# Fourier attention with routed experts: turning the phases of every step on TensorE from bfloat16 parts

## The chip, the cores and the metric

One NeuronCore of a Trainium2 chip runs the kernel. The metric is device time in microseconds (us), the median of 15 executions: 506.96 us before the change (504.1 to 509.99).

## The reference, cut to what matters

```python
# x: (8, 512, 128); 16 heads of 8; proj: (8, 128)
q = (x @ Wq.T + bq); k = (x @ Wk.T + bk); v = (x @ Wv.T + bv)
p = einsum('blhd,dm->blhm', q or k, proj) / sqrt(8)       # the phases
q_, k_ = concat([cos(p), sin(p)], -1) / sqrt(128)         # 256 features a head
kv = einsum('blhm,blhd->bhmd', k_, v); a = einsum('blhm,bhmd->blhd', q_, kv)
x = layernorm(x + a @ Wo.T + bo)
# 8 experts 128 -> 512 -> 128 with relu; each row goes to its best 2 of 8 by a softmax router
x = layernorm(x + sum_e routed[e] * (relu(x @ W1[e] + b1[e]) @ W2[e] + b2[e]))
```

## The kernel before, in words

**Attention.** A sequence (512 rows) is done in 8 steps: four make k features (one per chunk of 128 rows, all heads), four make q features (one per j of the four heads of each group of 32 channels, all rows). A step has 128 x 2048 phases in four banks of PSUM (`P4`, two halves `PH`), held by one step at a time. `p_phase` (line 546) multiplies a float32 block of 32 channels by the block-diagonal projection `pbd`, one matmul a bank, the four on four groups of 32 rows of the array. Phases are counted in turns, and must be brought to half a turn around zero before the sine. In a *turned* step (the first 24 of 64, `TURNED`, line 1476) TensorE does that: two bfloat16 matmuls a bank, `up` and `down`, add and take away a large constant (what is left is the phase rounded to whole turns), and the same float32 product with `npbd`, the negative projection, is added. `v_abs` on VectorE and `v_sin` on ScalarE then read PSUM, a half at a time. In the other 40 steps `p_phase` makes the product only; ScalarE adds the rounding constant (`v_round`, into the tile `r`), VectorE subtracts (`v_turn`), and absolute value (`v_absolute`) and sine (`v_sine`) are taken from `r` in SBUF, the whole step at once. In both, `v_cos` takes the cosine from the absolute value, in place. `products` (line 575) multiplies the features by v or by the summed kv.

**Experts.** After a sequence's attention come `v_aT`, `p_z`, `stats`, `Inverse` (power, then `newton`), the router (`v_route0` to `v_rank`), and GpSimd's indirect scatters of each row and its slot number into pages of 128 rows in DRAM (`ys`). Sequences 0 to 5 form group 0 (55 page loads), 6 and 7 group 1 (23). A page is loaded (`load`), its expert's W1, biases and shift row are loaded into one of six buffers of `wpool` (`weights`), and `p_hidden`, `v_max`, `p_answers`, `v_answers` and a scatter to `res` follow. When a group is done, `fetch`, `combine` (or `weigh` and `total`), a second layer norm and the store follow. Before rows are scattered, the pages are cleared from the tile `zero` (`clear`, line 279): 38 transfers of SP's queue, eight pages or fewer each.

**What sets the order.** Each engine works through its instructions in the order in which they are issued. `Plan.make` (line 1378) works that order out beforehand: a task has an engine, a cost in us, tasks that it waits for, buffers that it takes from rings, and a due time, shifted by the table `SHIFT`. Some tasks can go to either of two engines. The costs are numbers written in the code; nothing on the chip follows them except the order. SP's queue is also such an order: weights, pages, clears and stores wait behind one another.

Of the kernel before, what the change touches and what calls it, by code (L numbers as in the profile page):

```python
# [25 lines left out]
def kernel(  # L26
# [32 lines left out]
    P = 128  # L59
# [32 lines left out]
    wpool = ctx.enter_context(tc.tile_pool(name="wpool", bufs=6))  # L92
# [24 lines left out]
    first = feat.tile([P, NG * 512], F32, tag="r", name="first")  # L117
    wnat = first[:, 0 : 4 * D].rearrange("p (i d) -> p i d", d=D)
    for i, w in ((1, Wk), (0, Wq), (2, Wv), (3, Wo)):
        nc.scalar.dma_start(out=wnat[:, i, :], in_=w)  # L120
    proj_s = first[0:DH, 4 * D : 4 * D + M]
    sp.dma_start(out=proj_s, in_=proj)
    NB = E * NF
    brow = first[0 : NB + 3, 4 * D + M : 4 * D + M + P]
# [35 lines left out]
    pbd = const.tile([P, NJ * M], F32, name="pbd")  # L160


    npbd = const.tile([P, NJ * M], F32, name="npbd")
# [15 lines left out]
    )  # L179
    mm(P4[3][:, 0:M], heads, proj_s, start=True, stop=True)  # L180
# [11 lines left out]
    bqk = const.tile([P, 2], F32, name="bqk")  # L192


    def p_bcol(bank):
        tr(bank[:, 0 : NB + 3], brow, ident[: NB + 3, : NB + 3])

    def v_bcol(bank):
        dve.tensor_copy(bcol, bank[:, 0 : NB + 3])
        dve.tensor_scalar(bqk, bcol[:, NB : NB + 2], scale, None, ALU.mult)  # L200
# [19 lines left out]

    XW = D + DH
    vm = const.tile([P, NC, NJ * XW], F32, name="vm")
    pool.memset(vm, 0.0)
    kv = const.tile([P, 2, NJ * XW], F32, name="kv")
    pool.memset(kv, 0.0)
# [30 lines left out]
    DY = D + 1  # L258
    zero = const.tile([P, 8, DY], F32, name="zero")
    pool.memset(zero, 0.0)  # L260
    pool.memset(zero[:, :, D:DY].bitcast(I32), 1 << 30)
# [17 lines left out]
    def clear(i, e):  # L279
        n = full[i] if e + 1 < E else NT[i]  # L280
        for t0 in range(0, n, 8):
            k = min(8, n - t0)
            r0 = P * (full[i] * e + t0)
            sp.dma_start(
                out=ys_d[i][r0 : r0 + k * P, :].rearrange("(p k) d -> p k d", k=k),
                in_=zero[:, 0:k, :],
            )
# [56 lines left out]
    class Inverse:  # L344
# [5 lines left out]
        def tile(self, tag):  # L350
            return small.tile([P, NC], F32, tag=tag, name=f"{tag}_{self.name}")
# [8 lines left out]
        def newton(self, eng):  # L360

            rs, ve = self.rs, self.ve
            nw = self.tile("nw")
            eng.tensor_tensor(nw, rs, rs, ALU.mult)
# [61 lines left out]
    def v_rows(bank, r):  # L426
        if r == 0:
            rows8.append(feat.tile([P, NG * 512], F32, tag="r", name="rows8"))
        dve.tensor_copy(rows8[0][:, NG * r * D : NG * (r + 1) * D], bank)
# [7 lines left out]
    def prepare_shift():  # L437
# [10 lines left out]
        for r in range(E // NG):  # L448
# [3 lines left out]
                bank=("rows", r), free=("rows", r), ring=("r", "rows", 2),  # L452
# [3 lines left out]
        plan.give("r", "rows", [t], lag=5)  # L456
        return t

    wr_done, bcol_done = [], []

    def prepare_logits():
        t = plan.add("PE", 0.2, p_bcol, kind="p_bcol", due=-3.5, bank="bcol")
        b = plan.add("DVE", 0.45, v_bcol, kind="v_bcol", due=-3.4, after=[t], bank="bcol", free="bcol")
        bcol_done.append(b)
        t = plan.add("PE", 0.2, p_wo, kind="p_wo", due=-0.5, bank="wo")
# [5 lines left out]
    class Sequence:  # L471
        def __init__(self, b):
            self.b = b
            self.g = group_of(b)
            self.m = b - gstart[self.g.i]

            self.hurry = b >= B - 2
            self.xb = self.z = None

# [20 lines left out]
        def p_qk(self, i, bank):  # L500
            mm(bank, wT[:, i, 0:D], self.xT, start=True, stop=True)

        def v_qk(self, i, bank, eng):
            t = seq.tile(
                [P, L], F32, tag="qk"[i] + "T", name=f"{'qk'[i]}T_{self.b}", bufs=2 - i
            )
            if eng is dve:
                dve.tensor_scalar(
                    t, bank, bcol[:, NB + i : NB + i + 1], scale, ALU.add, ALU.mult
                )  # L510
            else:
                act.activation(t, bank, AF.Identity, bias=bqk[:, i : i + 1], scale=scale)
            if i:
                self.kT = t
            else:
                self.qT = t
# [29 lines left out]
        def p_phase(self, i, turned):  # L546
            for g in range(NG):
                r0 = 32 * g
                if i < NC:
                    lhs, rhs = self.kT[r0 : r0 + 32, ts(i)], pbd[r0 : r0 + 32, :]  # L550
                else:
                    lhs, rhs = pbd[r0 : r0 + 32, ts(i - NC)], self.qT[r0 : r0 + 32, :]
                mm(P4[g], lhs, rhs, start=True, stop=not turned)
# [13 lines left out]
            for g in range(NG):  # L567
                r0 = 32 * g
                if i < NC:
                    lhs, rhs = self.kT[r0 : r0 + 32, ts(i)], npbd[r0 : r0 + 32, :]  # L570
                else:
                    lhs, rhs = npbd[r0 : r0 + 32, ts(i - NC)], self.qT[r0 : r0 + 32, :]
                mm(P4[g], lhs, rhs, start=False, stop=True)
# [54 lines left out]
        def v_z(self, n, bank):  # L628
            if n == 0:
                self.z = seq.tile([P, NC, D + E], F32, tag="z", name=f"z_{self.b}")  # L630
                self.mv = small.tile([P, NC, 2], F32, tag="mv", name=f"mv_{self.b}")
# [181 lines left out]
        def start_out(self):  # L813
            self.mvo = small.tile([P, NC, 2], F32, tag="mvo", name=f"mvo_{self.b}")
# [5 lines left out]
        def prepare(self):  # L820
# [19 lines left out]
            self.t_k = add("PE", 1.0, lambda bank: self.p_qk(1, bank), kind="p_qk1", due=due + 1, after=[e] + ([before.t_p[NC - 1]] if b else []), bank=("k", b))  # L840
            self.k_done = add(
# [688 lines left out]
```

## Time and profile before

| what | us |
|---|---|
| median of 15 runs | 506.96 |
| the profiled execution, its own time | 507.4 |
| its span, first to last instruction | 505.3 |
| TensorE busy | 451.5 (89%) |
| VectorE busy | 397.9 (79%) |
| ScalarE busy | 358.1 (71%) |
| GpSimd busy | 278.7 (55%) |
| moved by DMA | 77.89 MB, mean 154 GB/s |

The views used here: the busy time of each engine in chosen stretches (columns: stretch, its length, then for each engine busy us and number of instructions, the granted TensorE clock, DMA share, GB/s); groups of instructions by form (count, then union of busy us, mean ns of one, and idle before); the timeline (start, length, engine, instruction, count of instructions merged in the line). PE is TensorE, PEld its weight loads, DVE VectorE, ACT ScalarE, POOL GpSimd, SP the engine that issues most DMAs. Ends of matmuls are modelled, so the cost of a piece of PE work is read from its start to the next piece's start. A float32 matmul shows as two matmul instructions, a bfloat16 one as one.

### The profile page before, as it was taken

How to read it: one execution, taken by the hardware profiler on the slowest of the kernel's cores; microseconds unless marked ns; L12 is line 12 of the kernel's file. 1: busy time of each engine (PE TensorE's matmuls, PEld its weight loads, DVE VectorE, ACT ScalarE, POOL GpSimd, SP SyncE). 2: the span in 40 equal slices, each digit the busy share in tenths (PEclk: the TensorE clock that was granted, in tenths of full speed). 3: DMA queues.
4: the chain of work that ended last, by engine and by line, in shares of the span. 5: the costliest groups of instructions: out<-in, count | busy, mean ns of one | idle time of the engine just before them, and what ended most of it. 6: DMA issues, size and time to landing. Idle time of an engine off the chain costs nothing.

```text
span 505.3 us, 13843 instructions
## 1 busy us (share of the span) xinstructions
PE 451.5 (89%) x5107; PEld 300.5 (59%) x5107; DVE 397.9 (79%) x910; ACT 358.1 (71%) x298; POOL 278.7 (55%) x490
## 2 busy tenths in 40 slices
PE   6999999999999999999999999999999697687910
PEld 3664564365267545764765567566657687687910
DVE  3845669579698999999999999999984564478884
ACT  3876887877899999999999999999992100011122
POOL 9300026526426862675577537764784577357685
PEclk9999999999999999999999999998999899899975
DMA  7999757301433035312531343027434576877631
GB/s 199 343 399 398 282 201 277 111 23 55 145 107 113 27 91 153 106 34 83 160 106 38 110 130 105 31 59 215 130 96 142 161 224 177 285 242 228 197 117 64
DMA packets 53110, 77.89 MB, mean 154 GB/s; under 512 B 7896, under 2 KB 31742, under 8 KB 53044
## 3 DMA queue, kind: packets, MB, share of 16 engines
q1 hardware_dynamic: 47604, 68.16, 42.8%
q0 software_dynamic: 4864, 8.60, 5.3%
q8 instruction: 41, 0.67, 0.6%
q10 hardware_dynamic: 576, 0.26, 0.2%
q14 instruction: 25, 0.20, 0.1%
HBM read 41.78 MB, written 34.02 MB: 150 GB/s over the span
## 4 chain that ended last, share of the span: by engine, by line
PE 57%; DVE 16%; ACT 8%; DMA 7%; issue 6%; POOL 4%; SPq 1%; POOLq 0%; ACTq 0%; DVEq 0%
PE bank L78 36%; PE p L78 21%; ACT f L78 4%; DVE r L78 4%; ACT r L78 3%; DMA wst<-wcat 3%; DVE f L78 2%; DVE hT L78 2%; DMA ys<-y,slot_i 1%; DMA got<-res 1%; DMA res<-og,yg 1%; DVE acc L78 1%; DVE st L78 1%; POOL rs_o L78 1%; DVE og L78 1%
## 5 line engine op out<-in xcount | busy, mean ns | idle before, releaser
L78 ACT ACTIVATE f<-f,halfpi 128x2048 f32<-128x2048 f32 x64 | 128.7, 2011 | 3.2 <-DVE f L78 1.2
L78 POOL DMA_INDIRECT res<-og,yg x78 | 86.5, 1108 | 70.6 <-DVE og L78 43.5
L78 DVE SCALAR_TENSOR_TENSOR r<-r,p 128x1024 f32<-128x1024 f32 x80 | 93.8, 1213 | 4.9 <-ACT r L78 4.8
L78 ACT ACTIVATE r<-p,magic 128x1024 f32<-128x1024 f32 x80 | 84.8, 1117 | 0.0
L78 DVE TENSOR_SCALAR f<-p 128x1024 int32<-128x1024 int32 x48 | 56.8, 1219 | 33.1 <-PE p L78 30.5
L78 POOL DMA_INDIRECT ys<-y,slot_i x64 | 69.5, 1085 | 22.3 <-issue 17.2
L78 ACT ACTIVATE f<-r 128x2048 f32<-128x2048 f32 x40 | 76.8, 1919 | 4.5 <-DVE r L78 3.5
L78 PEld LDWEIGHTS bank<-yTg,wst 128*128 128x128 f32 x464 | 57.4, 200 | 18.6 <-issue 6.8
L78 PEld LDWEIGHTS bank<-f,vm 128*32 128x32 f32 x2048 | 53.3, 110 | 24.0 <-issue 19.5
L78 PE MATMUL bank<-yTg,wst 128*128 128x128 f32 x464 | 63.5, 289 | 3.1 <-ACT yTg L78 1.6
L78 ACT ACTIVATE f<-p 128x1024 f32<-128x1024 f32 x48 | 49.1, 1024 | 23.9 <-PE p L78 17.0
L78 PE MATMUL bank<-f,vm 128*32 128x128 f32 x2048 | 64.2, 275 | 0.1
L78 POOL TENSOR_TENSOR xb<-x,bob 128x512 f32<-128x512 f32 x8 | 10.2, 1277 | 96.3 <-DVE z L78 96.3
L78 PE MATMUL bank<-w,hT 128*128 x464 | 60.8, 279 | 2.0 <-DVE hT L78 2.0
L78 PE MATMUL bank<-f,kv 128*32 128x512 f32 x512 | 61.9, 599 | 0.4 <-ACT f L78 0.4
L78 PEld LDWEIGHTS bank<-w,hT 128*128 128x128 f32 x464 | 55.6, 192 | 11.0 <-issue 4.1
L78 DVE TENSOR_SCALAR f<-r 128x2048 int32<-128x2048 int32 x40 | 49.0, 1225 | 0.1
L78 PE MATMUL p<-pbd,kT 32*128 32x512 f32 x256 | 44.2, 643 | 2.3 <-DVE r L78 1.0
L78 PE MATMUL p<-qT,pbd 32*128 32x512 f32 x256 | 43.4, 640 | 1.7 <-ACT f L78 1.7
L78 DVE TENSOR_TENSOR hT<-bank,wst 128x512 f32<-128x512 f32 x58 | 39.2, 683 | 3.0 <-PE p L78 1.2
L78 ACT ACTIVATE yTg<-bank 128x512 f32<-128x512 f32 (+1 forms) x13 | 7.6, 587 | 40.7 <-PE bank L78 40.7
L78 PEld LDWEIGHTS bank<-f,kv 128*32 128x32 f32 x512 | 13.3, 109 | 36.1 <-issue 25.4
(199 smaller groups left out, 625.9 us busy)
## 6 DMA issues: line engine op xcount, KB each, us to landing
wst<-wcat SPq DMA_DIRECT2D x78, 322.0 KB
ys<-zero SPq DMA_DIRECT2D x36, 516.0 KB
yg<-ys SPq DMA_DIRECT2D x78, 64.5 KB
got<-res SPq DMA_DIRECT2D x6, 512.0 KB
x<-in_L_attn_x_dram SPq DMA_DIRECT2D x8, 256.0 KB
wcat<-in_L_ffn_W_dram SPq DMA_DIRECT2D x8, 256.0 KB
w<-in_L_ffn_W_dram SPq DMA_DIRECT2D x8, 256.0 KB
acc<-y SPq DMA_DIRECT2D x8, 256.0 KB
```

What stands on the lines that cost most here:

```text
L78: ins = getattr(self.engine, op)(*args, **kwargs)
```

## The change

All 64 steps are turned. Except for the k steps of sequence 0 (`whole`), the projection is made from bfloat16 parts. `v_split` and `v_split2` write q or k as three bfloat16 parts that sum to it; the projection's parts are laid out once as `sproj` and `nsproj` in 64 rows: 8 products of parts by 8 channels of a head. For that the parts must stand in other rows: `store_parts` writes them to DRAM (two transfers), `load_parts` reads them back in runs of 24, 24 and 16 rows for each half of 64 (six transfers) as `rows_`. `project` then multiplies 64-row blocks, two halves of the array: four matmuls of 512 columns for a q step, sixteen of 128 columns for a k step, once with `sproj` and once with `nsproj`. Weight columns and biases of q and k are permuted to match (`wP`, `bperm`).

The tile `r` goes; `zero`, `first`, `rows8` and `pbd` move into the rings of other tiles, `wpool` has seven buffers. Clears go to GpSimd's queue, seven pages or fewer each (54 of them), planned four at a time by a ring of the plan. VectorE, not GpSimd, clears `vm`, `kv` and `zero` at the start. `newton` on VectorE takes four instructions and not six. The planner's costs, its rules for choosing among ready tasks and `SHIFT` are changed.

```diff
-    wpool = ctx.enter_context(tc.tile_pool(name="wpool", bufs=6))
+    wpool = ctx.enter_context(tc.tile_pool(name="wpool", bufs=7))
...
+    def split(eng, dst, src, left):
+        eng.tensor_copy(dst[:, 0, :], src)
+        eng.tensor_tensor(left, src, dst[:, 0, :], ALU.subtract)
+    def split2(eng, dst, left):
+        eng.tensor_copy(dst[:, 1, :], left)
+        eng.tensor_tensor(dst[:, 2, :], left, dst[:, 1, :], ALU.subtract)
...
+    vm = const.tile([P, NC, NJ * XW], F32, name="vm")
+    dve.memset(vm, 0.0)
+    kv = const.tile([P, 2, NJ * XW], F32, name="kv")
+    dve.memset(kv, 0.0)
+    zero = keep.tile([P, 7, DY], F32, tag="got", name="zero", bufs=3)
+    dve.memset(zero, 0.0)
...
-            sp.dma_start(
-                out=ys_d[i][r0 : r0 + k * P, :].rearrange("(p k) d -> p k d", k=k),
+    def clear(i, r0, k):
+        pool.dma_start(
+            out=ys_d[i][r0 : r0 + k * P, :].rearrange("(p k) d -> p k d", k=k),
+            in_=zero[:, 0:k, :],
+        )
...
+            if eng is dve:
+                self.nb = self.tile("nb")
+                dve.tensor_tensor(nw, rs, rs, ALU.mult)
+                dve.scalar_tensor_tensor(nw, nw, -0.5, ve, ALU.mult, ALU.mult)
+                dve.scalar_tensor_tensor(rs, nw, 1.5, rs, ALU.add, ALU.mult)
+                dve.scalar_tensor_tensor(self.nb, self.mv[:, :, 0], -1.0, rs, ALU.mult, ALU.mult)
+                return
...
+        def v_split(self, i, eng):
+            self.parts[i] = seq.tile(
+                [P, 3, L], BF16, tag="parts", name=f"{'qk'[i]}p_{self.b}", bufs=1
+            )
+            split(eng, self.parts[i], self.qk[i], self.qk[i])
+        def v_split2(self, i, eng):
+            split2(eng, self.parts[i], self.qk[i])
+        def store_parts(self, i):
+            self.parts_d[i] = tc.dram_tile([2, 3, P // 2, L], BF16, name=f"{'qk'[i]}p_d{self.b}")
+            for s in range(2):
+                sp.dma_start(
+                    out=self.parts_d[i][s].rearrange("m r n -> r m n"),
+                    in_=self.parts[i][64 * s : 64 * s + 64, :, :],
+                )
+        def load_parts(self, i):
+            t = seq.tile([P, 2 * NJ, L], BF16, tag="qk"[i] + "s", name=f"{'qk'[i]}s_{self.b}")
+            self.rows_[i] = t
+            src = self.parts_d[i].rearrange("s m (d t) n -> s (m d) (t n)", d=DH)
+            for s in range(2):
+                for n in range(3):
+                    k = min(3, NK - 3 * n)
+                    r0 = 64 * s + 24 * n
+                    sp.dma_start(
+                        out=t[r0 : r0 + 8 * k, :, :].rearrange("q t n -> q (t n)"),
+                        in_=src[s, 0 : 8 * k],
+                    )
...
+            self.project(i, pbd if self.whole(i) else sproj, True, not turned)
...
+            self.project(i, npbd if self.whole(i) else nsproj, False, True)
+        def whole(self, i):
+            return self.b == 0 and i < NC
+        def project(self, i, table, start, stop):
...
+            t = self.rows_[1 if i < NC else 0]
+            for G in range(2):
+                for j in range(NJ) if i < NC else (i - NC,):
+                    for s in range(2):
+                        at, k = slice(64 * s, 64 * s + 64), NJ * G + j
+                        if i < NC:
+                            mm(
+                                P4[2 * G + s][:, ts(j, M)], t[at, k, ts(i)], table[at, :],
+                                start=start and j == 0, stop=stop and j == NJ - 1,
+                            )
+                        else:
+                            mm(P4[2 * G + s], table[at, :], t[at, k, :], start=start, stop=stop)
...
+        def split(self, i, t, due):
+            t = add(
+                "POOL", 2.3, lambda: self.v_split(i, pool), kind="v_split", due=due, after=[t], ring=("parts", (b, i), 1),
+                other=("DVE", 1.1, lambda: self.v_split(i, dve)),
+            )
+            t = add(
+                "POOL", 2.3, lambda: self.v_split2(i, pool), kind="v_split2", due=due, after=[t],
+                other=("DVE", 1.1, lambda: self.v_split2(i, dve)),
+            )
+            s = add("SP", 0.8, lambda: self.store_parts(i), kind="store_parts", due=due, after=[t], land=2.6)
+            last = seqs[b - 1].t_p[NC - 1 if i else NS - 1] if b else None
+            return add("SP", 4.0, lambda: self.load_parts(i), kind="load_parts", due=due, after=[s, last] + sproj_done, land=4.5)
...
+                one_ = 1.14 if self.whole(i) else 0.65
                 p = add(
-                    "PE", 2.5 if turned else 1.1, s.p_phase, kind="p_phase", due=k,
+                    "PE", 2 * one_ + 0.2 if turned else one_, s.p_phase, kind="p_phase", due=k,
...
+                "POOL", 0.6, lambda i=i, r0=r0, k=k: clear(i, r0, k), kind=f"clear{i}",
+                due=0.3 * n + 8 * i, land=6, ring=("clear", n, 4),
...
-    HOP = 0.15
+    HOP = 0.07
-    SETUP = {"PE": 6.4, "ACT": 6.9, "DVE": 7.0, "POOL": 14.0, "SP": 17.0}
+    SETUP = {"PE": 5.75, "ACT": 6.8, "DVE": 6.7, "POOL": 11.6, "SP": 16.2}
+    WAIT = 0.2
+    EARLY = {"PE": 0.14, "ACT": 0.1, "DVE": 0.09, "POOL": 0.0, "SP": 0.0}
...
-TURNED = frozenset(range(24))
+TURNED = frozenset(range(64))
```

## The prediction

> **What bounds the kernel now.** I read the busy time by stretches first, since no mean over the span says what a change of one stage is worth. I cut the span where the turned steps end (136 us), where attention ends (379), and where the last matmul ends (482.6).
>
> ```profile
> 0.00:30.00 30.00, 24.86 (x324) 15.28 (x325) 17.08 (x29) 17.98 (x17) 16.35 (x83) 1.00 0.96 291
> 30.00:136.00 106.00, 104.35 (x1388) 53.61 (x1386) 74.18 (x155) 83.84 (x68) 34.64 (x68) 1.00 0.54 199
> 136.00:160.00 24.00, 22.75 (x287) 15.04 (x286) 20.48 (x37) 22.24 (x17) 9.75 (x18) 1.00 0.41 130
> 160.00:379.00 219.00, 215.44 (x2429) 137.10 (x2425) 207.17 (x421) 215.21 (x159) 138.23 (x192) 0.99 0.35 99
> 379.00:482.60 103.60, 84.10 (x693) 79.48 (x685) 65.51 (x216) 12.01 (x23) 64.14 (x92) 0.97 0.67 204
> 482.60:505.30 22.70, 0.00 (x0) 0.00 (x0) 13.47 (x56) 6.83 (x18) 15.64 (x38) 0.59 0.27 93
> ```
>
> The columns are PE, PEld, DVE, ACT, POOL, clock, DMA share, GB/s. Stage A (to 136, 24 turned steps) is PE's: 104.35 of 106.00 us, ACT at 79%. Stage B (136 to 379, 40 unturned steps) has PE at 98%, ACT at 98%, DVE at 94%. Stage C is the experts' tail: PE at 81%, DMA share 0.67. Stage D is the last layer norm and store.
>
> PE and ACT both look full in B; the groups by form tell which one leads.
>
> ```profile
> L78 ACT ACTIVATE f<-f,halfpi 128x2048 f32<-128x2048 f32 x64 | 128.7, 2011 | 3.2 <-DVE f L78 1.2
> L78 DVE SCALAR_TENSOR_TENSOR r<-r,p 128x1024 f32<-128x1024 f32 x80 | 93.8, 1213 | 4.9 <-ACT r L78 4.8
> ...
> L78 ACT ACTIVATE r<-p,magic 128x1024 f32<-128x1024 f32 x80 | 84.8, 1117 | 0.0
> L78 ACT ACTIVATE f<-r 128x2048 f32<-128x2048 f32 x40 | 76.8, 1919 | 4.5 <-DVE r L78 3.5 <-PE bank L78 0.8
> ...
> L78 DVE TENSOR_SCALAR f<-p 128x1024 int32<-128x1024 int32 x48 | 56.8, 1219 | 33.1 <-PE p L78 30.5 <-ACT f L78 2.5
> ```
>
> An unturned step costs ACT 2 x 1.117 + 1.919 + 2.011 = 6.16 us; 40 of them are 246 us, and B lasts 243 (neighbours overlap a little). ACT sets B. The PE timeline shows the price of both kinds of step, read from start to next start.
>
> ```profile
> 62.38 1.19 PE L78 MATMUL p<-pbd,kT 32*128 32x512 f32 x8
> 63.34 0.44 PE L78 MATMUL p<-up,once 32*128 32x512 bf16 x4
> 63.55 0.44 PE L78 MATMUL p<-down,once 32*128 32x512 bf16 x4
> 63.77 1.08 PE L78 MATMUL p<-npbd,kT 32*128 32x512 f32 x8
> 64.78 1.95 PE L78 MATMUL bank<-f,vm 128*32 128x128 f32 x64
> 66.67 0.73 PE L78 MATMUL bank<-wT,aT 128*128 128x136 f32 x4
> 67.33 1.14 PE L78 MATMUL p<-pbd,kT 32*128 32x512 f32 x8
> ```
>
> One float32 projection is 0.96 to 1.01 us; up and down together 0.43; a turned step's phases 62.38 to 64.78 = 2.40; its products 1.89; the period 4.95. In B the same form lasts longer, because it is held up between banks that ACT and DVE have not left:
>
> ```profile
> 255.81 2.15 PE L78 MATMUL p<-qT,pbd 32*128 32x512 f32 x8
> 257.89 2.05 PE L78 MATMUL bank<-yTg,wst 128*128 128x128 f32 x16
> ```
>
> The phases take 59.3 busy us in B (29.13 on qT, 30.18 on kT, the stretches of those tiles), against 40 x 1.14 = 45.6 when they run freely. So 13.7 us of PE's 238.2 in B are waits, and its work there is 224.5.
>
> **The change, part by part.** *New projections.* The trace has no matmul on 64 rows. For a q step, four matmuls of 512 columns run two at a time. The nearest row is up/down: four of 512 columns on four row groups in 0.215 us. Two pairs are then 0.43 (0.86 if the halves do not run together), and a q step is 0.43 + 0.43 + 0.43 = 1.29. For a k step, sixteen matmuls stream the same columns, 0.43, but each loads 128 columns of weights. Below: the products pay 1.89 / 64 = 29.5 ns for a matmul with its own load of 32 columns, 0.47 for sixteen. Above: the experts' float32 matmuls, full array, 128 columns loaded each, go eight in 0.89 us, 111 ns each, 1.78 for sixteen. I take 0.55, near the lower row, since loads into one half of the array can lie beside a matmul in the other, as up/down's four groups do: a k step is 2 x 0.55 + 0.43 = 1.53.
>
> The Trainium skill speaks against this ("TensorE: Matmul & The Clock Gate", "LDWEIGHTS (loading the stationary operand)"): a load costs its columns / 1.2 ns, however few its rows, 107 ns here. This trace's bfloat16 loads of 128 columns (`once`) average 93 ns, of the same size. By the page, with two halves loading side by side, sixteen would be an estimated 0.85 us, and the sum below some 17 us higher.
>
> *Stage A.* Four k steps of sequence 0 stay at 2.40. Of the other 20, eight are k steps (2.40 - 1.53 = 0.87 each) and twelve q steps (1.11 each): 7.0 + 13.3 = 20.3 us, all of it where PE is the limit. What is late next: ACT's 2 x 1.024 + 2.011 = 4.06 a step and the loop phases, two `v_abs` (2 x 1.219), phases, some 4.0. A's steps last (136 - 10)/24 = 5.25 us with their fillers, 4.40 afterwards, so both stay below. **-20.3.**
>
> *Stage B.* ACT loses 40 x (6.16 - 4.06) = 84 us and stops being the bound. DVE loses 40 x (2 x 1.213 + 1.225 - 2 x 1.219) = 48.5 of its 227.7 and gains the splits of ten tiles. A split is four passes of 128x512. The rows bound a pass between 0.31 (a quarter of the 1.225 us pass over 2048 elements in SBUF) and 0.68 (`hT`, 512 from PSUM); I take the code's 2.2 a tile, 22 us; DVE falls to 201. On GpSimd a pass is 1.28 (`xb`, 128x512); it is busy 148 of 243 in B and has room. PE becomes the bound: 20 k steps x (1.53 - 0.97) + 20 q steps x (1.29 - 0.97) = +17.6; 224.5 + 17.6 = 242.1. At the packing of A (104.35/106, 98.4%) that takes 246 us against 243. **+3.** So the 84 us of ACT buy almost nothing here: the bound moves over to PE, which was nearly full.
>
> *Start.* q of sequence 0 is needed at step 4, 30.6 us. Its parts go behind the loads on SP's queue (last issued at about 18 us) while DMA runs at a share of 0.96. Store and load are 0.39 + 1.05 MB; nearby landings are 3.1 us (`res`) and 5.7 (the chain's longest `got`). 18 + 3.1 + 5.7 = 27 at best; doubled under load, 36. A stall of 0 to 5; I take **+2**. VectorE's memsets cost GpSimd 1.97 + 1.06 + 1.02 before; DVE waits for the projection until 4.8 us anyway, so they are hidden there; without that cover, up to 2.
>
> *Later returns.* 15 tiles x 1.44 MB = 21.6 MB on 77.9; DMA share is 0.54 in the rest of A, 0.35 in B. A tile may load as soon as its predecessor's four steps are over, and has the other kind's four steps, 16 us, to land. SP gets 120 issues of 0.4 to 0.7 us (48 to 84) and loses 38 clears of 1.2 us (46). Nothing, as long as SP's order holds; behind a waiting `load_parts` stand the weights of the next pages, whose seven buffers cover some 15 us.
>
> A second rule speaks against it ("DMA: Bandwidth & Descriptors", "Why a DMA increments its semaphore by 16 and not by 1"): a transfer uses the largest number of engines up to 16 that divides its rows, so 12 for 24 rows. No run here shows it yet. By it four of the six transfers would last a third longer, an estimated 2 us on a 5.7 us landing, inside the 16 us of cover.
>
> *Clears.* 54 on GpSimd at 0.6 (its plain transfers: 522 to 614 ns) are 32 us, most between 20 and 60 us, where GpSimd is busy 0.00 and 0.00. Nothing; in another place they would hold scatters.
>
> *Tail.* Two waits on the weights in the chain of C are 5.9 and 5.0 us; a seventh buffer lets a load start one page sooner (103.6/38 = 2.7 us): 0 to -5.4, I take -3. The shorter `newton`, once on the last chain, -0.4. **-3.4.**
>
> Sum: 507.4 - 20.3 + 3 + 2 - 3.4 = 488.7 on the profiled execution's own time, which stands 0.1% above the median of 506.96. **Forecast 489.**
>
> **Rivals.** (1) *The loads of the k steps' weights are the bound.* 28 k steps x 2 projections. From 57 ns a matmul (0.91 a projection) the gain is gone: 28 x 2 x 0.36 = 20. Halfway between both rows, 72 ns, 1.16 a projection: 28 x 1.22 = +34, **523**, slower than before. For it: 111 ns is the only row with loads of 128 columns for each matmul. Against: those are float32 and hold the whole array. (2) *The parts come back late.* SP's fixed order meets landings longer than planned, 1 us more for each of 14 returns and 5, not 2, at the start: 488.7 + 14 + 3 = **506**, no change to measure. For it: DMA at 0.96 at the start, chain waits of 5 to 6 us on weights. Against: 16 us of cover. (3) *Splits hold PSUM.* 30 half splits of 1.1 us stand in DVE's order before a `v_abs`, which alone frees PSUM for the next phases; if a quarter shows on PE, +8: **497**. For it: DVE at 94% in B. Against: GpSimd has room, and DVE falls to 201. (4) *PE's slack in C closes too.* Held-back pages fill the 19.5 us that PE idles there, and ACT's freedom lets B run at 100%: 489 - 4 - 10 = **475**.
>
> **How the numbers follow.** Forecast 0.50 (480 to 499), (1) 0.14, (2) 0.10, (3) 0.10, (4) 0.16. About 0.3% is what a measurement can tell from no change. Faster: 0.50 + 0.16 + 0.10 and a little of (2), 0.78; same 0.04, slower 0.18 from (1) and the rest of (2). The range reaches to (4) and past (2), with all low ends (0.43 a projection -6.7, start -2, tail -2.4, and part of (4)) giving 470, and the break-even of (1) plus half its price 514.
>
> **What would show it.** Mean steps of 4.4 us in A instead of 5.25; phases of a q step at 1.3 and of a k step at 1.5 from start to start (above 2.2: rival 1); ACT below 75% and PE above 97% in B; attention ending near 360; no PE idle that a `qs` or `ks` load ends (else 2); no PE wait on a split (else 3). Wrong altogether if PE's work grows by more than 20 us or SP's queue holds the weights.

## The result, and the profile after

The changed kernel takes **537.9 us** (median of 9 runs, 534.6 to 539.9) against 506.4 (46 runs): a ratio of **1.062** (95% interval 1.060 to 1.064). The forecast was 489 with a range to 514: the change was to make the kernel faster, and made it slower. The profiled span is 535.3 us, 30.0 more than before. Some runs of a kernel are slower than others without a reason that a trace gives; ratios, and the differences worked out from them, leave out runs over 1.5% above the fastest of their kernel, medians do not.

The page of the kernel after, first its busy times and then the rows of TensorE's busy share and of DMA (40 slices, tenths):

```profile
PE 454.6 (85%) x5943; PEld 306.4 (57%) x5943; DVE 375.0 (70%) x912; ACT 293.4 (55%) x275; POOL 298.5 (56%) x539
...
PE   5985998959974999999998999999989999789700
...
DMA  7998799595489945674556467423787776859131
```

ScalarE lost 65 us and VectorE 23, as the change promises; TensorE is as busy as before (451.5) and idles 27 us more. The stretches, cut where attention (366 us) and the last matmul (509.1) end now; columns as in the prediction (PE, PEld, DVE, ACT, POOL, clock, DMA share, GB/s):

```profile
0.00:30.00 30.00, 22.57 (x175) 12.86 (x175) 18.28 (x44) 10.69 (x10) 20.75 (x99) 1.00 0.94 301
30.00:136.00 106.00, 88.31 (x1478) 48.21 (x1472) 71.58 (x141) 78.11 (x66) 53.56 (x97) 0.92 0.82 235
136.00:160.00 24.00, 21.84 (x274) 8.85 (x271) 16.89 (x37) 19.64 (x17) 12.09 (x16) 1.00 0.62 163
160.00:366.00 206.00, 193.37 (x2981) 113.98 (x2981) 170.83 (x386) 161.93 (x132) 115.29 (x185) 0.98 0.59 144
366.00:509.10 143.10, 128.54 (x1048) 122.46 (x1046) 84.49 (x252) 14.64 (x30) 82.04 (x106) 0.98 0.68 208
509.10:535.30 26.20, 0.00 (x1) 0.00 (x0) 12.94 (x54) 8.40 (x22) 14.78 (x38) 0.56 0.25 90
```

Stage A, 104.35 of 106 us busy before, is down to 88.31, at a DMA share of 0.82 instead of 0.54 and a granted clock of 0.92 instead of 1.00. Attention ends only 13 us sooner, and by its end 17 of the 78 pages are begun (40 at its end before), so the tail lasts 143 us, not 104.

From the trace, each matmul's time up to the start of the next (gaps apart) gives an account of TensorE that adds up to the span. `base` is the best repaired version of the experiments below.

| us | before | after | base |
|---|---|---|---|
| phases | 114.1 | 114.1 | 112.8 |
| products, pages, all other matmuls | 337.4 | 340.6 | 339.0 |
| idle between first and last matmul | 27.0 | 50.4 | 41.3 |
| ahead of the first and behind the last matmul | 26.9 | 30.3 | 30.4 |
| span | 505.3 | 535.3 | 523.5 |

So there are two questions. Why did the phases not get cheaper (the prediction's steps make them 114.1 - 20.3 + 17.6 - 13.7 = 97.7)? And where do 23.4 us of new idle time come from?

**The phases.** TensorE's timeline of the kernel after, a q step and a k step with what follows each:

```profile
219.37 0.61 PE L78 MATMUL p<-qs,sproj 64*128 64x512 bf16 x4
219.91 0.39 PE L78 MATMUL p<-up,once 32*128 32x512 bf16 x4
220.13 0.38 PE L78 MATMUL p<-down,once 32*128 32x512 bf16 x4
220.45 0.60 PE L78 MATMUL p<-qs,nsproj 64*128 64x512 bf16 x4
220.99 1.95 PE L78 MATMUL bank<-f,vm 128*32 128x128 f32 x64
...
237.96 0.62 PE L78 MATMUL p<-sproj,ks 64*128 64x128 bf16 x16
238.51 0.40 PE L78 MATMUL p<-up,once 32*128 32x512 bf16 x4
238.74 0.38 PE L78 MATMUL p<-down,once 32*128 32x512 bf16 x4
239.05 0.62 PE L78 MATMUL p<-nsproj,ks 64*128 64x128 bf16 x16
239.60 1.92 PE L78 MATMUL bank<-f,kv 128*32 128x512 f32 x16
```

From start to start a q step is 220.99 - 219.37 = 1.62 us (predicted 1.29) and a k step 1.64 (predicted 1.53). Four matmuls of 512 columns and sixteen of 128 with their own loads cost the same 0.54, and `down` takes 0.32 where `up` takes 0.22.

**The idle time.** The longest pieces of DMA within attention, in the chain of waits that ended last (start, length):

```profile
24.40 12.30 DMA qp_d<-qp
...
38.70 7.54 DMA qs<-qp_d
...
106.94 4.79 DMA kp_d<-kp
...
150.53 13.72 DMA kp_d<-kp
```

All four belong to the parts. The first two are the return of q of sequence 0: stored at 24.4, landed at 36.7, loaded by 46.2. TensorE waits 3.73 and 2.68 us for it. The other two are only *stores*, whose data no one reads at that moment. Why they hold TensorE shows in the timeline around 110 us (all engines, shortened):

```profile
106.29 1.26 SPq L78 DMA_DIRECT2D kp_d<-kp  x2
...
108.68 0.62 PE L78 MATMUL p<-nsproj,ks 64*128 64x128 bf16 x16
...
111.94 0.43 DVE L78 CAST qp<-qT 128x512 bf16<-128x512 f32 x1 [5.21 <-DMA kp_d<-kp]
112.41 0.69 DVE L78 TENSOR_TENSOR qT<-qT,qp 128x512 f32<-128x512 f32 x1
113.13 0.43 DVE L78 CAST qp<-qT 128x512 bf16<-128x512 f32 x1
113.60 0.69 DVE L78 TENSOR_TENSOR qp<-qT,qp 128x512 bf16<-128x512 f32 x1
114.20 2.35 DVE L78 TENSOR_SCALAR f<-p 128x1024 int32<-128x1024 int32 x2
...
115.46 1.02 ACT L78 ACTIVATE f<-p 128x1024 f32<-128x1024 f32 x1 [5.03 <-DVE f L78]
...
116.53 1.03 PE L78 MATMUL p<-sproj,ks 64*128 64x128 bf16 x16 [6.24 <-ACT f L78]
```

Read it from the bottom. TensorE waits 6.24 us for PSUM, which ScalarE's sine leaves late, because that sine and the `v_abs` (`f<-p`) take turns on the halves. `v_abs` stands in VectorE's order behind the split of q; and the split waits 5.21 us for the *store of k's parts*, since the tile `parts` has one buffer, which may be overwritten only when that store has landed. A buffer's way out has become a wait in the order of the engine that frees PSUM. The same holds at 160 us, where the split waits 10.09 us for a store of k and TensorE 7.90:

```profile
164.34 0.43 DVE L78 CAST qp<-qT 128x512 bf16<-128x512 f32 x1 [10.09 <-DMA kp_d<-kp]
...
167.73 1.03 PE L78 MATMUL p<-sproj,ks 64*128 64x128 bf16 x16 [7.90 <-ACT f L78]
```

### The profile page after: what moved, and what is told of

Its sections match the earlier page's. It is cut to its first block, busy times and chain, and to the rows that moved or that the text cites. A ratio compares the mean times of both kernels' runs of the same rounds, so it can differ in the third digit from the quotient of the medians.

```text
span 535.3 us, 15649 instructions
## 1 busy us (share of the span) xinstructions
PE 454.6 (85%) x5943; PEld 306.4 (57%) x5943; DVE 375.0 (70%) x912; ACT 293.4 (55%) x275; POOL 298.5 (56%) x539
## 4 chain that ended last, share of the span: by engine, by line
PE 61%; DVE 14%; DMA 11%; issue 5%; POOL 4%; ACT 2%; SPq 2%; POOLq 0%; DVEq 0%; ACTq 0%
PE bank L78 36%; PE p L78 25%; DVE f L78 4%; DMA kp_d<-kp 3%; DVE hT L78 2%; DMA qp_d<-qp 2%; ACT f L78 2%; DMA res<-og,yg 2%; DMA qs<-qp_d 1%; SPq L78 1%; POOL res L78 1%; POOL rs_o L78 1%; DVE og L78 1%; DMA got<-res 1%; DVE acc L78 1%
## 5 line engine op out<-in xcount | busy, mean ns | idle before, releaser
L78 DVE TENSOR_SCALAR f<-p 128x1024 int32<-128x1024 int32 x128 | 154.1, 1220 | 35.6 <-PE p L78 32.4
L78 ACT ACTIVATE f<-p 128x1024 f32<-128x1024 f32 x128 | 129.4, 1021 | 65.6 <-PE p L78 32.2
L78 POOL DMA_INDIRECT ys<-y,slot_i x64 | 62.6, 978 | 31.6 <-issue 20.3
L78 PE MATMUL bank<-yTg,wst 128*128 128x128 f32 x376 | 51.9, 281 | 3.5 <-issue 2.9
L78 PEld LDWEIGHTS bank<-yTg,wst 128*128 128x128 f32 x376 | 46.2, 193 | 9.6 <-issue 8.1
L78 PEld LDWEIGHTS <-ks 64*128 64x128 bf16 x896 | 26.9, 97 | 37.3 <-issue 35.3
L78 PE MATMUL p<-w,hT 128*128 x248 | 35.2, 291 | 10.0 <-DVE hT L78 9.5
L78 PEld LDWEIGHTS p<-w,hT 128*128 128x128 f32 x248 | 30.9, 199 | 13.6 <-DVE hT L78 12.9
L78 PE MATMUL p<-sproj,ks 64*128 64x128 bf16 x448 | 18.3, 224 | 15.7 <-ACT f L78 15.7
L78 DVE TENSOR_TENSOR hT<-p,wst 128x512 f32<-128x512 f32 x31 | 21.1, 687 | 15.0 <-PE p L78 13.1
L78 PE MATMUL p<-yTg,wst 128*128 128x128 f32 x248 | 31.1, 276 | 0.0
L78 POOL DMA_DIRECT2D ys<-zero x54 | 29.6, 554 | 2.7 <-DMA ys<-y,slot_i 1.5
## 6 DMA issues: line engine op xcount, KB each, us to landing
ys<-zero POOLq DMA_DIRECT2D x38, 451.5 KB, 7.9
```

The source lines that it names most:

```text
L78: ins = getattr(self.engine, op)(*args, **kwargs)
```

## The experiments

The theory after this reading: the idle time is the parts' way through DRAM, by the one buffer and by transfers that the clears delay. The rivals: single causes at the start (the return of q of sequence 0, the memsets), and TensorE's work itself, which did not fall.

**Four kernels on a slower chip.** These four ran on a chip on which the kernel before takes 531.9 us, and the kernel after was not among them; only their order among each other counts. Three take one suspect away from the kernel after each; the fourth undoes the parts and keeps all 64 steps turned (its order is planned anew). The edits are shown cut, `...` for lines left out.

```diff
 # held_source: every later load reads sequence 0's stored q parts
-            src = self.parts_d[i].rearrange(...)
+            held = seqs[0].parts_d[0] if self.b else self.parts_d[i]
+            src = held.rearrange(...)
 # moved_clears: after plan.make(), group 0's clears later in the order
+    for n, t in enumerate(moved):          # tasks of kind "clear0"
+        t.start = max(t.start, 36.0 + 1.25 * n)
+    plan.order.sort(key=lambda t: t.start)
 # memsets_back
-    dve.memset(vm, 0.0)
+    pool.memset(vm, 0.0)
...
 # f32_turned: no parts; float32 blocks of 32 rows in every step
-            return self.b == 0 and i < NC
+            return True
...
```

> Every load of parts from sequence 1 on reads the DRAM tile that q of sequence 0 was stored to, not its own (so all later sequences compute with sequence 0's q rows); bytes, issues and the order on every engine stay, only the wait of a load for its own store goes. Theory R (the returns through DRAM come too late): the gaps of TensorE that end in a ks load, 6.2 us at 110 and 7.9 at 160 and some shorter ones, go; 16 us less, about 522. Theory W (TensorE simply has more work, and a gap closed is paid for later): within 3 us of 538.

> The 38 clears of group 0 keep their form but stand later in GpSimd's order, spread over the plan's time from 36 to 82 us, behind the store and load of q of sequence 0; all other orders stay. Theory R with the clears as the cause (they fill the DMA engines while the first parts are under way): the store of q of sequence 0 lands in about 4 us and not 12.3, step 4 starts some 10 us sooner, about 527. Theory R with the queue as the cause (the parts stand behind 4 MB of weights and x in SP's own queue): step 4 no more than 3 us sooner, about 535. Theory W: 538.

> vm, kv and zero are cleared by GpSimd again. If the 4.2 us by which the first phase starts later (14.5 against 10.2) come from VectorE's memsets, the first phase starts near 11 us and the time falls by 3 to 4 us, to 534. If the first returns decide the start anyway (theory R: q of sequence 0 lands at 46 us whatever TensorE does before), the first phase moves and the time stays within 1.5 us of 538.

> The parts are undone alone: all 64 steps are turned, each with float32 projections as in the k steps of sequence 0; no splits, no stores or loads of parts; the planner orders anew. A float32 turned step takes TensorE 2.40 us, one from parts 1.63: 60 x 0.77 = 46 us more work, and some 25 us of waits on returns less. Theory R and W both: 538 + 46 - 25 = 559. If the parts cost more than they give (waits and all else over 46 us), below 538.

Measured: 594.8, 593.9, 595.5 and 637.2 us; ratios to the kernel before 1.118 (1.111 to 1.126), 1.117 (1.108 to 1.127), 1.118 (1.111 to 1.125) and 1.200 (1.191 to 1.208). The first three can't be told apart. In `held_source` no load from sequence 1 on waits for its own store, and yet the two long waits of TensorE stay (9.6 us to 120 us, 5.9 us to 172 us): it is not the return of the parts that they wait for. In `moved_clears` step 4 comes some 10 us sooner than in `held_source` (its cosine at 41.7 us, not 52.5), and the gain is lost again at 102 us, where TensorE waits 11.4 us instead of 9.6: one late wait was only the first of several. In `memsets_back` the first cosine comes later (25.6 us against 18.7), because GpSimd, busy with the memsets, issues the load of `Wr` later. `f32_turned` shows what the parts are worth to TensorE: its phases take 171.2 us in the account above against 118.7 in `held_source`, 52.5 us, and 42 us of that are in the time (about 20 more than the kernel after were expected), though a new order has its share in that. The parts do make a turned step cheaper. Why this chip punishes the changed kernel by 12% is open; in `held_source` TensorE idles 86 us in the account and its mean granted clock is 0.917 (50 us and 0.950 in the kernel after).

**The buffer and the clears.** On a chip that takes 506.0 us for the kernel before: the kernel after again, then a second buffer for the parts with the order kept (two small tiles moved elsewhere and a buffer that the plan does not use given up, to make room), then also the clears later.

```diff
 # parts2
-                [P, 3, L], BF16, tag="parts", name=f"{'qk'[i]}p_{self.b}", bufs=1
+                [P, 3, L], BF16, tag="parts", name=f"{'qk'[i]}p_{self.b}", bufs=2
 # parts2_moved2: parts2 and, after plan.make()
+    for kind, first, step in (("clear0", 36.0, 1.25), ("clear1", 250.0, 2.0)):
+        for n, t in enumerate(t for t in plan.order if t.kind == kind):
+            t.start = max(t.start, first + step * n)
+    plan.order.sort(key=lambda t: t.start)
 # mix2: parts2_moved2, planned anew with every third step unturned
-TURNED = frozenset(range(64))
+TURNED = frozenset(k for k in range(64) if k % 3 != 2)
```

> The changed kernel itself, as the measure for the runs beside it: the chip of the four runs before took 531.9 us for the kernel before the change, where the first chip took 506.4. If the extra time of those runs is the chip's, this one stands as far above the kernel before as the runs with small edits did, a ratio of 1.12 there or 1.06 as at first; if the edits made it, 1.06 on any chip.

> The tile parts has two buffers and not one (paid for with a buffer that the plan does not use and two small tiles moved); all orders stay. Theory P: the gaps of 6.2 us at 110 and 7.9 at 160 come from a split in VectorE's order, which must wait until the store of the previous parts has landed, with the v_abs that frees PSUM queued behind it; both gaps go, 14 us less than the changed kernel. Theory R (the load's own return is late): the gaps stay, less than 3 us gained. Theory I (TensorE waits for its instructions): stay as well.

> As parts2, and the clears of group 0 stand later in GpSimd's order (plan time 36 to 82 us), those of group 1 at plan time 250 and later; all other orders stay. If the clears are what makes stores and loads of parts late, step 4 starts 8 to 10 us sooner, as in moved_clears, and nothing is lost at 110: 22 us less than the changed kernel. If DMA is short of time whichever transfers go first, no more than parts2.

> As parts2_moved2, and every third step is unturned (21 of 64; the products of a step are kept behind those of the step before; the planner orders anew). An unturned step from parts takes TensorE 0.6 us and not 1.63, so 21 us less work, and gives ScalarE 21 x 2.1 = 44 us, VectorE 25 us more, which had 45% and 30% to spare. Theory W (TensorE's work is the bound): 15 to 20 us less than parts2_moved2. If waits decide, within 5 us of it, or above by what the new order costs.

Measured: 541.0 us, 1.071 (1.064 to 1.077); 532.9, 1.050 (1.043 to 1.056); 527.7, 1.033 (1.025 to 1.040); 613.7, 1.215 (1.208 to 1.222). By the ratios the second buffer is worth some **10 us** (2.1% of 506; the two intervals do not touch), where 14 were expected. VectorE's timeline of `parts2` has the split of q with no wait for a store and behind two `v_abs`, not before them; TensorE's next projection stands below.

```profile
106.60 1.22 DVE L78 TENSOR_SCALAR f<-p 128x1024 int32<-128x1024 int32 x1 [0.91 <-PE p L78]
108.02 1.22 DVE L78 TENSOR_SCALAR f<-p 128x1024 int32<-128x1024 int32 x1 [0.19 <-ACT f L78]
109.16 0.42 DVE L78 CAST qp<-qT 128x512 bf16<-128x512 f32 x1
109.61 0.69 DVE L78 TENSOR_TENSOR qT<-qT,qp 128x512 f32<-128x512 f32 x1
```

```profile
113.89 0.29 PE L78 MATMUL p<-sproj,ks 64*128 64x128 bf16 x4 [1.23 <-ACT f L78]
```

TensorE's wait there falls from 6.9 us (in `after_again`) to 1.2. The later clears are worth another **8 or 9** (1.7%; again the intervals do not touch): by its packets the store of q of sequence 0 lands in 3.2 us instead of the 12.3 above, and step 4's cosine is at 44.4 us instead of 52.2 in `after_again`. `mix2` says nothing of the phases: its order is a new one, by due times that were fitted to other work, and two waits of 17 us for pages appear near the end.

**Is it TensorE's work?** `base` is `parts2_moved2` once more, as a control. `base_no_round` leaves out the matmuls `up` and `down` of 60 steps, `base_mix4` makes 15 steps unturned at the places of the turned steps' own instructions (in `v_abs` and `v_sin`, not shown), both with the order of `base`.

```diff
 # base_no_round
-            for t in (up, down):
+            for t in (up, down) if self.whole(i) else ():
 # base_mix4
-                s = Step(self, i, turned)
+                s = Step(self, i, turned and not (k >= 7 and k % 4 == 3))
 # before_less_cos (the kernel before; in base_less_cos n = 1024 in every step)
-            act.activation(f[:, 1, :], f[:, 1, :], AF.Sin, bias=halfpi, scale=-TWO_PI)
+            n = 2048 if self.turned else 1024
+            act.activation(f[:, 1, 0:n], f[:, 1, 0:n], AF.Sin, bias=halfpi, scale=-TWO_PI)
 # before_less_abs: before_less_cos, v_absolute on 1024 columns, and ahead of the cosine
+                act_copy(f[:, 1, n:], self.r[:, n:])
```

> The kernel of parts2_moved2 once more (a second buffer for the parts, clears of group 0 from 36 us and of group 1 from 250 us on), as the control of the next two on one chip. Every theory: the same ratio to the kernel before as it had, 1.025 to 1.04 on a chip that takes some 506 us for the kernel before; its waits of over 1 us at the return of q of sequence 0 (1.7 us), at 105 us (3.5 us) and its two waits without a releaser (2.6 and 3.4 us) again.

> The control with one thing left out and the same order: the eight matmuls up and down of the 60 steps made from parts. The phases then cancel (the sine is of 0, the cosine 1), so the output is not the reference's. The trace shows them at 0.54 us a step between the two projections, 32 us in all. Theory W (TensorE's work is what is left of the bound, so each us of it is a us of the span): 24 to 32 us below the control, steps shorter by 0.5 us each, ratio to the kernel before 0.96 to 0.985. Theory I (what is left is waits that other engines and transfers set): 0 to 12 us below, and TensorE's idle time grows by what its busy time loses. A side reading: with both projections one after the other, in the same mode, eight matmuls of 512 columns should take 0.86 us if a change between 64 and 32 rows costs time (the trace had 0.54 + 0.54 beside up and down) and 1.08 if the 0.54 is the matmuls' own.

> The control with 15 of the 60 steps (every fourth from step 7 on) unturned: one projection from parts on TensorE, the rounding on ScalarE and VectorE as the kernel before does it, put at the places of the turned step's own instructions, so the order of everything else is kept. TensorE loses 15 x (1.65 - 0.55) = 16 us; ScalarE gains 15 x 2.1 = 32 us at 55% of its span, VectorE 15 x 1.2 = 18 us at 71%. Theory W: 8 to 16 us below the control. Theory I or a new wait (the next step's phases wait for PSUM until the rounding behind a cosine of 2 us is over): 0 to 15 us above it.

> The control of the runs beside it: the second buffer for the parts and the later clears, as before. 1.03 to 1.045 of the kernel before.

> The control with the cosine of every step taken of the first 1024 of 2048 columns only, so the output is not the reference's. ScalarE loses 64 x 1.0 us, its floor under a step falls from 4.2 us (the steps of the run without up and down came no closer than 4.2) to 3.2; TensorE keeps all its work. Theory W (TensorE's work sets attention after the returns are repaired): 0 to 3 us below the control. Theory I (ScalarE's loop sets it): 15 us or more below.

> The control with both left out: the matmuls up and down of 60 steps (32 us of TensorE) and half of each cosine (64 us of ScalarE), so the output is not the reference's. Without up and down alone 9 us went. If ScalarE's loop of 4.2 us stood right behind TensorE, now 20 to 30 us go. If the returns, the order and the transfers are what is left, it stays at 8 to 14 us.

Measured, on one chip: `base` 528.1 us (four runs from 519.2 to 534.1), `base_no_round` 518.7 with 1.022 (1.016 to 1.027), `base_mix4` 576.1 with 1.138 (1.133 to 1.142); the kernel before 507.3. On another: `base2` 529.9 with 1.045 (1.038 to 1.053), `base_less_cos` 521.8 with 1.027 (1.019 to 1.036), `base_less_both` 512.6 with 1.008 (1.005 to 1.011); the kernel before 507.9.

Taking `up` and `down` from TensorE gives between 4 us (518.1 against the mean of 522.2 of the two runs of `base` that count) and 9 us (the medians): theory I either way. Taking 64 us from ScalarE gives 9 (neither theory: between the two), taking both gives 18 (again between the two ranges). As far as the scatter of the control tells, the two about add. So neither is *the* bound of the repaired kernel; the reading is that some steps are TensorE's and others ScalarE's. Turned steps come no closer than 4.2 us in `base` and `base_no_round`, 3.5 in `base_less_cos` and 2.8 with both left out. The account of `base_no_round` shows where TensorE's gain went: phases 37.2 us less than in `base` (changes of shape go too), its other matmuls 15 us more (held up within the products, and at a mean granted clock of 0.944 instead of 0.965), idle time 57.0 us instead of 41.3. `base_mix4` is a miss, some 50 us slower. Its timeline around step 15:

```profile
103.92 2.00 ACT L78 ACTIVATE f<-f,halfpi 128x2048 f32<-128x2048 f32 x1
...
105.83 2.10 ACT L78 ACTIVATE f<-p,magic 128x1024 f32<-128x1024 f32 x2
105.98 0.16 PEld L78 LDWEIGHTS bank<-f,kv 128*32 128x32 f32 x8 [1.41 <-ACT f L78]
105.98 1.06 PE L78 MATMUL bank<-f,kv 128*32 128x512 f32 x8 [0.51 <-ACT f L78]
106.96 2.35 DVE L78 SCALAR_TENSOR_TENSOR f<-f,p 128x1024 f32<-128x1024 f32 x2 [2.41 <-ACT f L78]
```

The rounding (`f<-p,magic`) reads PSUM only when ScalarE is done with the cosine of the step before (2.00 us), then VectorE reads it too. So an unturned step holds PSUM longer, an estimated 3 us (48 us between the medians, over 15 steps); that is a reading from this one step. This is where turning on TensorE helps.

`base_no_round` also prices the phases. With the two projections one after the other:

```profile
222.15 0.62 PE L78 MATMUL p<-sproj,ks 64*128 64x128 bf16 x16
222.61 0.61 PE L78 MATMUL p<-nsproj,ks 64*128 64x128 bf16 x16
223.15 2.19 PE L78 MATMUL bank<-f,kv 128*32 128x512 f32 x16
```

A projection followed by its like is 222.61 - 222.15 = 0.46 us (0.43 for most q steps of this run), one followed by another shape 0.54. The matmuls' own time is what the prediction took for a q step (0.43); each change of shape, three in a step's phases, adds 0.08 to 0.11 (`down` 0.32 against `up` 0.22 likewise). The Trainium skill names a reason ("TensorEngine Tiling (Array Packing)", "Key Properties"): changing the tiling mode, not just the tile, drains the engine; it gives no price, and no run here tells such a drain from a weight load that can't be hidden.

**What set the kernel before.**

> The kernel before with less of one thing: in its 40 unturned steps the cosine is taken of the first 1024 of 2048 columns only, so the output is not the reference's. ScalarE loses 40 x 1.0 = 40 us of its 6.16 a step, nothing else changes. The prediction's reading of stage B (ScalarE sets it, and TensorE with 224.5 us of work in 243 is close behind): 10 to 18 us below the kernel before, ratio 0.965 to 0.98. Rival (TensorE sets stage B already, and its long phases are matmuls slowed by something else than a wait for ScalarE): 0 to 5 us below, 0.99 to 1.0. Rival (ScalarE alone sets it, and the phases' waits close and more besides): 30 to 40 us, 0.92 to 0.94.

> The kernel before with less on VectorE: in its 40 unturned steps the absolute value is taken of the first 1024 columns only, ScalarE copies the other 1024 (1.1 us) and leaves their cosine out (1.0 us), so the output is not the reference's, ScalarE's time is the same and VectorE loses 40 x 0.61 = 24 us. Half the cosine alone moved nothing (0.999), so ScalarE does not set stage B. If VectorE does (94% busy there): 8 to 20 us below the kernel before, 0.96 to 0.985. If TensorE does: 0 to 3 us below, 0.995 to 1.0, and TensorE's long float32 phases of 2.1 us stay.

Measured: `before_less_cos` 506.0 us against 507.3, 0.999 (0.996 to 1.001); `before_less_abs` 504.7 against 507.9, 0.995 (0.992 to 0.998). The stretch from 160 to 377 us, in stage B, first in the kernel before:

```profile
160.00:377.00 217.00, 213.44 (x2412) 135.75 (x2405) 205.17 (x419) 213.21 (x158) 136.54 (x191) 0.99 0.35 100
```

in `before_less_cos`, with ScalarE's sine:

```profile
160.00:377.00 217.00, 213.41 (x2421) 135.85 (x2413) 206.31 (x420) 186.45 (x159) 137.04 (x191) 1.00 0.36 100
```

```profile
L78 ACT ACTIVATE f<-r 128x2048 f32<-128x2048 f32 x37 | 70.7, 1912 | 30.3 <-DVE r L78 24.3 <-PE bank L78 3.7 <-PE p L78 2.1
```

and in `before_less_abs`:

```profile
160.00:377.00 217.00, 213.09 (x2434) 135.78 (x2437) 189.89 (x421) 216.92 (x195) 123.83 (x193) 1.00 0.36 100
```

With half a cosine less ScalarE falls from 98% to 186.45 of 217 us and idles 30.3 us at its sine; nothing gets sooner. With less absolute value VectorE falls from 95% to 189.89; the kernel gets 3 us sooner, within what was expected if TensorE sets the stage. TensorE stays at 213 of 217 in all three. So neither ScalarE alone nor VectorE alone set stage B. What is left is TensorE, in the order that it was given, but not TensorE's work alone: from start to next start the phases of the 40 unturned steps take 56.5 us (57.0 and 54.2 in the two runs), where 40 free ones of 1.07 take 42.8. So 11 to 14 us of waits for PSUM stand inside TensorE's busy time and stay there whichever engine is relieved. Relieving both at once in the kernel before was not tried.

## Why the prediction was wrong, step by step

The step that failed first is "Later returns: nothing, as long as SP's order holds", an overlap that was not there; with it "Clears: nothing", and the new projections, a term that was mis-sized.

- **New projections.** Mis-sized: 1.62 and 1.64 us a step instead of 1.29 and 1.53. 32 q steps x 0.33 + 28 k steps x 0.11 = 13.6 us. What failed was the reading that matmuls on 64 rows and on 32 rows can be priced apart and added: the change of shape has a price of its own. The 128-column loads, rival (1), cost next to nothing: a k step's projection is 0.55, a q step's 0.54, and the estimate from the Trainium skill ("TensorE: Matmul & The Clock Gate", "LDWEIGHTS (loading the stationary operand)": 0.85, 17 us in all) does not come out here, where sixteen loads of 97 ns each lie within 0.45 us.
- **Stage A, -20.3.** The steps that wait for nothing do take 4.2 to 4.6 us, as forecast (4.40). But the 24th cosine starts at 149.9 us, not 135.9. Up to there the account has 10.2 us less of phases (some 5 of the forecast 20.3 are the mis-sized projections, some 5 more are phases at half rate, see below), 4.8 us more of other matmuls, and 21.8 us of idle time instead of 2.7: the start, the return of q, the wait that ends at 116.5 us and smaller ones.
- **Stage B: "ACT sets B", +3.** That ScalarE set it is not borne out: half a cosine less moved nothing. That TensorE is then the bound was right in its terms and wrong in their sizes. The 13.7 us for which TensorE's phases were held did go: 57 of the 60 steps from parts take 1.61 to 1.73 us. But its work grew by 20 x 0.57 (k: 1.64 against the 1.07 of a free step) + 20 x 0.55 = 22 us, not 17.6, and one step ran at half clock; the phases of stage B grew from 56.5 to 66.6 us, by 10.1 and not by 17.6 - 13.7 = 3.9. Idle time there grew by 9.2, most of it the wait of 7.9 us for a store. The remark that the 84 us of ScalarE buy almost nothing was right, though not because ScalarE had been the bound.
- **Start, +2.** Mis-sized. q of sequence 0 was back at 46 us, beyond the 36 called "doubled under load"; its store alone took 12.3 us (3.2 with the clears later), and its load, issued at 36.7, another 9.5; by their packets all loads of parts take 8 to 13 us, where the longest landing that I went by was 5.7. The start itself is 4.2 us later too (first phase at 14.5 us, before 10.2). VectorE's memsets, said to be hidden, stand before its copies and are 1.6 us of it (the first projection from `xT` at 8.83 us instead of 7.22), and memsets on GpSimd were no better; the rest is mostly matmuls (11.28 to 14.47 us) that stood behind the first phases before. In the profiled execution the first step then runs at half rate (its phases take 4.58 us instead of 2.36; the first record of a full clock is at 20.7 us).
- **Later returns: "nothing, as long as SP's order holds".** False, and the largest piece: about 14 us of TensorE's idle time in two waits of 6.2 and 7.9, of which the second buffer gave some 10 back. I had counted the cover of the *load* (16 us) and never asked what waits for the *store*. Rivals (2) and (3) each had half of it: late transfers, and splits ahead of `v_abs`. Neither joined them by the one buffer, and 14 returns of 1 us were in truth three waits of 6 to 8. The trace does not tell which engines a transfer ran on, so the rule on 24 rows (12 of 16 engines) stays untested.
- **Clears: "nothing".** They cost 8 or 9 us in the place they were given. GpSimd was free, but the 16 DMA engines were not (share 0.94 in the first 30 us), and the store of q landed 9 us later than with the clears put off.
- **Tail, -3.4.** Not seen by itself. The stretch behind the last matmul grew from 22.8 to 26.2 us. In the trace GpSimd's last DRAIN instruction, behind which the program ends, lasts 8.09 us (526.35 to 534.44; the last DMA packet has landed by 529.2) and lasted 3.68 (500.84 to 504.52) in the kernel before. Every run with the clears on GpSimd's queue, 206 DMA issues of GpSimd in all, has 8.09, `f32_turned` without parts too; every run of the kernel before, with 152, has 3.68. So these 4.4 us are most likely one more price of the clears on that queue; no run moves them back alone. Rival (4), pages drawn into attention, went the other way: 17 pages instead of 40.

Together: phases 16.4 us above the forecast (114.1 against 97.7), idle time 23.4 above before, the end 3.4, other matmuls 3.2. The sum of the last three with phases unchanged is the 30 us. Of the 16.4 us, some 14 are the mis-sized projections and 6.6 phases at half rate (the first step and the steps right after the three long waits), less 4 because a free unturned step had cost 1.07 us and not 0.97.

Still open after the repairs: `base` is 18 us of span above the kernel before, of which 14 are idle time of TensorE in many pieces under 4 us, and 3.4 the end. Nearest to an answer are the 4 to 9 and the 9 us above, and the DMA engines: in `base` the clears stand later, and the load of parts issued at 76.8 us lands at 103.9, 27 us later (loads take 8 to 13 us in the kernel after), with TensorE waiting for it. Leaving the clears out altogether was not tried, since unwritten pages would then be read. No version here beats the kernel before.

## What to carry to other kernels

For every buffer that a change sends out by DMA, ask who waits until it has *left*, and what stands behind that waiter in its engine's order; here one missing buffer put a store of 5 to 14 us between VectorE and PSUM. An engine at 98% is not thereby the bound, and its busy time can hold waits: leave out some of its work, in the order given, and see whether anything moves. Before TensorE is given more work to free another engine, price each change of tile shape with it.

## What the hardware showed besides

- **A wait can cost TensorE twice.** The granted clock can fall to half after it. The stretches that follow the three long waits of the kernel after (at 46.3, 116.5 and 167.7 us; the clock stands ahead of the DMA share):

```profile
46.30:49.30 3.00, 2.92 (x19) 0.45 (x23) 0.30 (x1) 0.00 (x0) 0.00 (x0) 0.50 0.96 365
...
116.50:119.50 3.00, 2.97 (x41) 1.74 (x40) 0.36 (x2) 2.36 (x2) 2.21 (x4) 0.50 1.05 343
...
167.70:170.70 3.00, 2.97 (x44) 1.73 (x47) 2.62 (x11) 2.00 (x1) 2.10 (x4) 0.50 0.96 287
```

  The phases right after take 2.9 us (46.38 to 49.25, though one of the matmuls came before; 167.73 to 170.64) instead of 1.62 and 1.65. In `base`, a wait of 2.43 us at 102 us was followed by a clock of 0.52, one of 1.73 us at 39 us by 1.00 (the rows in order of time):

```profile
40.60:42.00 1.40, 1.34 (x14) 0.32 (x13) 0.00 (x1) 1.36 (x1) 0.00 (x0) 1.00 0.89 195
...
105.30:108.00 2.70, 2.70 (x36) 1.25 (x35) 2.34 (x5) 0.25 (x1) 1.64 (x2) 0.52 0.94 198
```

  The Trainium skill ("TensorE: Matmul & The Clock Gate", "Part 1: The HAM clock gate (the "warmup" mystery)") gives half rate after an idle window of some 3.4 us; the half agrees. The length of a wait alone does not settle it here: in `base2` 1.47 us were enough (0.50 from 41.0 to 44.3 us), and 2.90 us in the kernel after, at 292 us, left the clock at 1.00.
- **Runs of 8 KB are slow on the way back.** The trace's packets of the returning parts, 8192 bytes, take 614 ns (13.3 GB/s an engine); most of the clears' packets, 7224 bytes, take 311 ns (23.3), the clears of the kernel before, most of 4128 bytes, 169 ns (24.4). 1920 such packets are 1920 x 0.614 / 16 = 74 us of all 16 engines, where the bytes at the clears' rate would be 42. Whether the direction, the size or the load of the engines makes the difference was not separated.
